# Four convolution layers in one kernel: layer 2's edge columns and masks from GpSimd to ScalarE, and its difference one quarter earlier

## The chip, the cores and the metric

The kernel runs on one core of a Trainium2 chip. The metric is the device time of one execution in microseconds (us), the median of several runs. Engines are named as in the profile: PE is TensorE's matrix products and PEld its weight loads, DVE is VectorE, ACT is ScalarE, POOL is GpSimd, SP is SyncE, which here only issues transfers.

## The reference

The input x has 16 images of 64 channels of 128 x 128 points, float32. Four layers follow each other, each of the form x + layer(gn(x)), where gn normalizes groups of two channels to mean 0 and variance 1:

- layer 0: the Gram matrix of the normalized channels, applied to them, then a 64 x 64 matrix
- layer 1: the absolute values of a horizontal and a vertical 3 x 3 Scharr filter of each channel, summed
- layer 2: a 3 x 3 convolution, 64 to 64 channels, with bias, of an input in which the first 16 channels are shifted one column to the left and the next 16 one column to the right (zeros come in at the edge)
- layer 3: a 3 x 3 and then a 1 x 1 convolution, batch normalization over all 16 images, a clip to 0..255

```python
x = x + _L0_conv_ref(_gn(x), L0_conv_conv_w)
x = x + _L1_conv_ref(_gn(x))
x = x + _L2_conv_ref(_gn(x), L2_conv_W, L2_conv_b)
x = x + _L3_conv_ref(_gn(x), L3_conv_w_bin, ...)
```

## The kernel before

The images go through the layers as a pipeline. One image is cut into eight chunks (NS = 8); a chunk is eight rows of each half of the image for layer 1, and eight pairs of rows for layers 2 and 3. A **step** handles one chunk of each of three images at once: `Front` is layers 0 and 1 of one image, `Layer2` and `Layer3` are those of images some ten steps further back, and `Gram` gathers the Gram matrix of an image still to come. So eight steps make a **cycle**, in which the whole pipeline advances by one image. `starts` gives the step in which each stage begins (15, 25, 35). `both_layers(step)` is true for the steps in which both layer 2 and layer 3 have work.

Each step has four quarters, q = 0 to 3, and within a quarter the stages are called in the order Layer3, Layer2, Front, then `section()` emits TensorE products that are held back, and then "last of q" parts of Layer2 come. All engines are wrapped in `InOrder`: what the program writes first for an engine is what that engine does first. So a call's place in this loop is its place in its engine's queue. The waits between engines are put in by the tile framework.

Layer 2 treats pairs of rows, so that 3 rows x 2 outputs become fewer products. For chunk i+1, in step i:

- `load` brings the rows by six transfers on SyncE's queue into v (tag v2, three buffers). The shift of 32 channels by a column is done by where the transfer reads.
- In quarter 1 ScalarE normalizes them (`v<-v,co` in the profile, 128 x 1154). The shifted channels have wrong columns at the edges. GpSimd first saves what layer 2 has to add at the first and the last column (`edges`, four instructions of 64 x 8), then multiplies both edge columns of v by masks (`keep0`, `keep1`; `v<-v,kc`, two instructions of 128 x 9 or 8).
- `different(i + 1)` lets VectorE form the difference of even and odd rows, d2 (`d2a<-v` and `d2b<-v`, 128 x 1024; two buffers in turn), and GpSimd then issues two transfers that copy d2 into q2, in the other half of the partitions and moved by one column (`q<-d2a`, `q<-d2b`; one buffer). Before step 34 it also copies into the same half, with four transfers.

In step i+1 TensorE uses them: `shared` (quarter 2) multiplies the odd rows into `one` (`one<-v,wi`, a PSUM tile with a single buffer, which layer 3's `one<-v,w` uses in turn); `own` (quarter 3) multiplies d2 into `two` (`two<-d2a,wi`, two buffers, shared with layer 3). `apart_across`, emitted by `section()` of the step before (quarter 1), multiplies q2 into `two`: the products `two<-q,pk` and `two<-q,cross`. They alternate in pairs with layer 3's `two<-d,w`, on other quarters of the array, and the products `po<-x,abd` of layer 0 follow them.

ScalarE adds the bias in reading `one` out (`c<-one,co` for layer 2, `c<-one,b_sb` for layer 3), which frees `one`. VectorE adds the edge columns (`two<-two,edges`) and reads `two` out (`x<-two,c` for layer 2, `y<-two,c` for layer 3), which frees `two`. Of layer 1, VectorE does ten operations per chunk (names u and e), with two Abs by ScalarE between; the last two are `u<-xh,co,u` in quarter 2 and `u<-e,co,u` in quarter 3.

VectorE's order in a full step, before: `u<-xh`, `e<-xh`, `two<-two,edges`, `x<-two,c`, four operations on u and e, `y<-two,c`, layer 3's difference `d<-v`, `u<-xh,co,u`, `u<-e,co,u`, layer 2's difference `d2<-v`. Small operations that work out coefficients stand between them.

Of the kernel before, what the change touches and what calls it, by code (L numbers as in the profile page):

```python
# [11 lines left out]
AF = mybir.ActivationFunctionType  # L12
# [3 lines left out]
B, C, H, W = 16, 64, 128, 128  # L16
# [4 lines left out]
R = 8  # L21
NS = HH // R
# [87 lines left out]
def tile_kernel(ctx: ExitStack, tc: tile.TileContext, x, cw_h, w2_t, b2, wbin_t, w1_t, b1, gamma, beta, consts, out):  # L110
    nc = tc.nc
    pe, dve, act, sp, pool = (InOrder(tc, e) for e in (nc.tensor, nc.vector, nc.scalar, nc.sync, nc.gpsimd))
# [8 lines left out]
    def k(name):  # L121
        return kc[:, AT[name][0]:AT[name][1]]
# [47 lines left out]
    last = [1]  # L170
# [52 lines left out]
    for name in ("d2a", "d2b", "q2", "d3"):  # L223
        t = wpool.tile([P, 2, CP, W + 2], F32, name=name)
# [42 lines left out]
    now = [0]  # L267
# [29 lines left out]
    def coefficients(st, put, back=None):  # L297

        yield
        yield from when(TENSOR)  # L300
        pm = sm(2 * NS)
        small_product(pm, k("gmean"), st.rearrange("p a n -> p (a n)"))
        yield
        co = sv("co", 2) if back is None else sv("co2", 6)
        me = sv("me", 2)
        r, mean = co[:, 0:1], me[:, 0:1]
        yield from rstd(pm, r, me, GN_EPS, None if back is None else co[:, 2:3])
        pool.tensor_scalar(co[:, 1:2], mean, r, -1.0, op0=ALU.mult, op1=ALU.mult)
        if back is not None:

            pool.tensor_add(co[:, 5:6], mean, back)
            pool.tensor_mul(co[:, 3:4], co[:, 2:3], k("left"))
            pool.tensor_mul(co[:, 4:5], co[:, 2:3], k("right"))
        put(co)
# [135 lines left out]
    rows = []  # L450
# [36 lines left out]
    class Gram:  # L487
        first, last = 2, NS + 2
# [4 lines left out]
        def at(self, i, q):  # L493
            b = self.b
            n = 4 * (i - NS) + q

            self.part({1: 44, 5: 42, 9: 42}.get(n, 0))
            if n == 10:
                chains.append(gram_chain(b, self.pg))

            if i == 2 and q == 0:
                for m in range(3):
                    self.load(m)
            m = {11: 0, 13: 1, 15: 2, 19: 3, 21: 4, 23: 5, 27: 6, 31: 7}.get(4 * i + q)
            if m is not None:
                rows_to_columns(b, m, self.xr.pop(m))
                if m + 3 < NS:
                    self.load(m + 3)
# [45 lines left out]
    class Front:  # L554
        first, last = -3, NS
# [182 lines left out]
    def both_layers(step):  # L738

        return starts[0][1] <= step < starts[1][1] + NS * B  # L740
# [60 lines left out]
    def apart_across(two, table, q, m):  # L801

        for kx in range(3):
            for n in range(2):
                o, i = single(table, n)
                w = W - 1 if kx == 2 else W
                wt = cross[cols(1 - i), kx - 1] if kx else packed["pk2"][cols(1 - i), n]
                across.append((
                    two[cols(o), n, 0:m, 0:w], wt, q[cols(1 - i), n, 0:m, kx + 1:kx + 1 + w], kx == 0, kx == 2,
                ))  # L810
# [3 lines left out]
    class Layer2:  # L814
        first, last = -2, NS
# [68 lines left out]
        def at(self, i, q):  # L884
            b = self.b
            closing = i + 1 == NS
            m = CP - 1 if closing else CP
            if q == 0:
                if i == NS:
                    chains.append(coefficients(self.st, self.done))  # L890
                if 1 <= i:
                    two = self.p.pop(i - 1)[0]

                    e = self.edges.pop(i - 1).rearrange("p t (m n) -> p n m t", n=2)
                    ends = two[:, :, :, 0:W:W - 1]
                    dve.tensor_add(ends, ends, e)
                    x3 = ring.tile([P, 2, CP, W], F32, tag="x3", name=f"x3_{b}_{i - 1}", bufs=NS + 2)
                    tiles3[b].append(x3)
                    dve.scalar_tensor_tensor(
                        x3.rearrange("p s j w -> p s (j w)"), two.rearrange("p s j w -> p s (j w)"), 1.0,  # L900
                        self.c.unsqueeze(1).to_broadcast([P, 2, CP * W]),
                        op0=ALU.mult, op1=ALU.add, accum_out=self.st[:, 0, i - 1:i],
                    )
            if q == 1:
                if i == 0:

                    self.wi = stp.tile([P, 2, 3, P], F32, tag="wi", name=f"wi_{b}", bufs=1)
                    for n, base in ((0, w2[:, 2]), (1, wm)):
                        dve.scalar_tensor_tensor(
                            self.wi[:, n].rearrange("p k o -> p (k o)"), k("I3"), self.co[:, 2:3],  # L910
                            base.rearrange("p k o -> p (k o)"), op0=ALU.mult, op1=ALU.add,
                        )
                if -1 <= i < NS - 1:
                    if i == -1:
                        self.co = coefs2.pop(b)
                    t, f = self.v[i + 1], self.whole.pop(i + 1)
                    act.activation(f, f, AF.Identity, bias=self.co[:, 1:2], scale=self.co[:, 0:1])


                    e = stp.tile([P, 2, R], F32, tag="edges", name=f"edges_{b}_{i + 1}", bufs=3)  # L920
                    for side, at in ((0, 0), (1, W + 1)):
                        for rows, j in ((lo, 1), (hi, 0)):
                            n = at + j * W
                            pool.tensor_scalar_mul(
                                e[rows, side], f[rows, n:n + (R - 1) * W + 1:W], self.co[rows, 3 + side:4 + side]
                            )
                    self.edges[i + 1] = e

                    pool.tensor_scalar_mul(t[:, :, 0], t[:, :, 0], k("keep0"))
                    pool.tensor_scalar_mul(t[:, :, W - 1], t[:, :, W - 1], k("keep1"))  # L930
                if i + 2 < NS:
                    self.load(i + 2)
                if 0 <= i < NS:
                    self.two = ps_two.tile([P, 2, CP, W], F32, tag="two", name=f"two2_{b}_{i}")
                    if both_layers(now[0]):
                        apart_across(self.two, TO_SLOTS, q2, m)
            if q == 2:
                if 0 <= i < NS:
                    t = self.v[i]
                    one = ps_one.tile([P, CP, W], F32, tag="one", name=f"one2_{b}_{i}")  # L940
                    two = self.two
                    self.p[i] = two, one
                    shared(one, self.wi[:, 0], t, m)
                    if closing:
                        small_product(one[:, m, :], w0, t[:, R, :])


                if 1 <= i < NS:
                    self.square(i - 1)
                if 1 <= i:  # L950
                    self.store(i - 1)
            if q == 3:
                if 0 <= i < NS:
                    t = self.v.pop(i)
                    two, one = self.p[i]
                    both = self.wi[:, 1]
                    for n in range(2):
                        own(
                            two[:, n], n, TO_SLOTS, w2, d2[i % 2], packed["pk2"],
                            None if both_layers(now[0]) else q2, m, both,  # L960
                        )
                    if closing:
                        p = two[:, 1, m:CP]
                        issue([taps(0, p, [both], [t[:, R:R + 1, :]]), taps(1, p, [both], [t[:, R - 1:R, :]])])
                        p, srcs = two[:, 0, m:CP], [t[:, R - 2:R - 1, :], t[:, R - 1:R, :]]
                        issue([taps(0, p, [w2[:, 0], both], srcs), taps(1, p, [both, w2[:, 1]], srcs)])
            if q == "last of 2" and 0 <= i < NS:
                self.c = ring.tile([P, CP * W], F32, tag="c2", name=f"c2_{b}_{i}", bufs=1)
                act.activation(self.c, flat(self.p[i][1]), AF.Identity, bias=self.co[:, 5:6])
            if q == "last of 0" and i == NS:  # L970
                self.square(i - 1)
            if q == "last of 3" and -1 <= i < NS - 1:
                self.different(i + 1)


    class Layer3:
        first, last = -1, NS
# [142 lines left out]
    for step in range(starts[2][1] - 2, steps):  # L1120
        now[0] = step
        for q in range(4):
            for b in range(B):

                i = step - starts[2][1] - NS * b
# [11 lines left out]
            for b in range(1, B):  # L1137
                at, n = pace[b]
# [28 lines left out]
            if step >= last_one and q == 2:  # L1167

                n = 3 if step == last_one else 1 if step < last_one + NS - 2 else 0
# [29 lines left out]
    e = cpool.tile([P, 1], F32, name="e_bn")  # L1199
# [56 lines left out]
```

## Time and profile before

| | us |
|---|---|
| median of 3 runs | 2649.29 |
| lowest and highest | 2647.46, 2650.26 |
| the profiled execution | 2646.72 |
| its span in the profile | 2645.0 |
| start, until both layers run | 0 to 350 |
| full pipeline with Gram products | 350 to 1583 |
| full pipeline without them | 1583 to 1968 |
| layers 2 and 3 without Front, then layer 3 alone | 1968 to 2200 |
| end: batch normalization and output | 2200 to 2645 |

All engine instructions stand under one line, L73, the helper that records them, so groups are told apart by what they write and read: `out<-in`. A group's row gives the number of instructions, busy time, the mean of one in ns, and the idle time of the engine just before them. A wait's row gives the total, the number of times and the longest. A timeline row gives the start, the duration, and in brackets the idle time of the engine before it with what ended it.

### The profile page before, as it was taken

The numbers are of one execution on the slowest core, as the hardware profiler recorded it, in microseconds if no ns is written. First come the engines' busy times: TensorE is split into PE (matmuls) and PEld (weight loads), VectorE is DVE, ScalarE is ACT, GpSimd is POOL, SyncE is SP. The second block draws the span as 40 slices with busy tenths as digits, with TensorE's granted clock in tenths as the row PEclk, the third lists the DMA queues.
The fourth block names the chain that finished last, engine by engine and source line by source line (L and its number), as shares of the span: only waits on it lengthen the run. The fifth ranks groups of instructions, "written<-read, shape, count | busy, mean of one in ns | idle before, by whom it ended". The sixth has DMA issues, their size and how long they took to land.

```text
span 2645.0 us, 46238 instructions
## 1 busy us (share of the span) xinstructions
PE 2086.3 (79%) x15748; PEld 832.0 (31%) x15748; DVE 2090.4 (79%) x2759; ACT 1787.3 (68%) x2529; POOL 993.3 (38%) x1391
## 2 busy tenths in 40 slices
PE   6568899999999999999999999999999991000000
PEld 4334333434343434343443433333333330000000
DVE  4998899999999999999999999999993335333332
ACT  4766678787878787877878777777774475333332
POOL 3365545343445454444445355555553100000000
PEclk8689899999999999999999999999999995555555
DMA  8799979898888889888979777787767769999999
GB/s 202 204 240 229 222 196 235 209 231 223 231 224 224 221 222 228 218 230 211 238 206 249 196 202 201 193 206 202 208 172 181 204 202 377 419 419 418 419 418 369
DMA packets 682267, 654.53 MB, mean 247 GB/s; under 512 B 56320, under 2 KB 576672, under 8 KB 682032
## 3 DMA queue, kind: packets, MB, share of 16 engines
q1 hardware_dynamic: 668208, 613.83, 80.3%
q0 software_dynamic: 13824, 37.75, 5.5%
q8 instruction: 126, 2.06, 0.3%
q14 instruction: 109, 0.89, 0.1%
HBM read 346.23 MB, written 268.44 MB: 232 GB/s over the span
## 4 chain that ended last, share of the span: by engine, by line
PE 38%; DMA 19%; DVE 2%; ACT 2%; SPq 2%; issue 1%; POOL 0%; DVEq 0%; ACTq 0%; POOLq 0%
PE two L73 21%; PE one L73 13%; SPq L73 2%; PE po L73 2%; PE bank L73 2%; DMA end_x<-x_d 2%; DMA xw<-x_d 2%; DMA xw<-y_d 2%; DMA end_x<-y_d 2%; DMA out<-end_x 2%; DMA out<-xw 1%; DMA out<-end_v 1%; DMA end_u<-x_d 1%; DMA d2b<-y_d 1%; DMA v<-x_d 1%
## 5 line engine op out<-in xcount | busy, mean ns | idle before, releaser
L73 PE MATMUL two<-d,w 64*64 64x512 f32 (+2 forms) x2992 | 697.5, 594 | 0.0
L73 POOL TENSOR_SCALAR edges<-v,co 64x8 f32<-64x8 f32 x512 | 364.2, 711 | 499.6 <-ACT v L73 314.0
L73 PE MATMUL one<-v,w 128*64 128x508 f32 (+2 forms) x1600 | 358.0, 579 | 0.3
L73 PE MATMUL one<-v,wi 128*64 128x508 f32 (+3 forms) x1536 | 353.6, 595 | 0.1
L73 PEld LDWEIGHTS two<-d,w 64*64 64x64 f32 (+1 forms) x2992 | 204.6, 134 | 391.5 <-issue 379.1
L73 DVE SCALAR_TENSOR_TENSOR e<-e 128x1032 f32<-128x1032 f32 (+1 forms) x256 | 313.1, 1223 | 0.0
L73 ACT ACTIVATE xh<-po,co 128x128 f32<-128x128 f32 (+1 forms) x480 | 274.6, 621 | 28.8 <-PE po L73 24.3
L73 PE MATMUL two<-q,cross 64*64 64x508 f32 (+3 forms) x944 | 244.8, 574 | 0.0
L73 PE MATMUL po<-x,abd 64*64 64x512 f32 (+1 forms) x1024 | 205.6, 623 | 48.7 <-ACT xh L73 43.4
L73 DVE SCALAR_TENSOR_TENSOR y<-two,c 128x1024 f32<-128x1024 f32 x128 | 156.0, 1219 | 97.9 <-ACT junk L73 44.7
L73 POOL TENSOR_SCALAR v<-v,kc 128x9 f32<-128x9 f32 x256 | 218.0, 866 | 12.0
L73 ACT ACTIVATE u<-u 128x1024 f32<-128x1024 f32 x128 | 135.3, 1057 | 127.9 <-DVE u L73 127.8
L73 ACT ACTIVATE v<-x,co 128x1024 f32<-128x1024 f32 (+3 forms) x256 | 203.1, 842 | 0.0
L73 ACT ACTIVATE v<-v,co 128x1154 f32<-128x1154 f32 x128 | 171.8, 1342 | 34.4 <-DMA v<-x_d 30.5
L73 DVE TENSOR_TENSOR d<-v 128x1024 f32<-128x1024 f32 x128 | 157.5, 1230 | 47.0 <-ACT v L73 29.2
L73 ACT ACTIVATE c<-one,co 128x512 f32<-128x512 f32 x128 | 87.6, 685 | 157.4 <-PE one L73 156.9
L73 PE MATMUL two<-q,pk 64*64 64x512 f32 (+2 forms) x512 | 175.9, 600 | 14.4 <-DMA q<-d2b 7.9
L73 DVE SCALAR_TENSOR_TENSOR u<-xh 128x1170 f32<-128x1170 f32 x128 | 175.4, 1371 | 10.6 <-DMA x_d<-u 5.4
L73 PE MATMUL two<-d2a,wi 128*64 128x508 f32 (+1 forms) x768 | 183.2, 589 | 0.0
L73 PE MATMUL two<-d2b,wi 128*64 128x508 f32 (+3 forms) x768 | 174.9, 566 | 0.0
L73 PEld LDWEIGHTS one<-v,w 128*64 128x64 f32 x1600 | 111.5, 136 | 190.2 <-issue 172.0
L73 DVE SCALAR_TENSOR_TENSOR u<-xh,co,u 128x1024 f32<-128x1024 f32 x128 | 164.1, 1282 | 8.5 <-ACT u L73 8.5
(174 smaller groups left out, 3744.7 us busy)
## 6 DMA issues: line engine op xcount, KB each, us to landing
x<-in_x SPq DMA_DIRECT2D x256, 256.0 KB, 4.1
x_d<-u SPq DMA_DIRECT2D x512, 128.0 KB, 3.8
y_d<-y SPq DMA_DIRECT2D x512, 128.0 KB, 3.4
x_d<-x SPq DMA_DIRECT2D x496, 128.0 KB, 3.2
xr<-in_x SPq DMA_DIRECT2D x120, 512.0 KB, 5.7
v<-x_d SPq DMA_DIRECT2D x448, 72.1 KB, 2.8
v<-x_d SPq DMA_DIRECT2D x224, 144.2 KB, 2.8
end_x<-x_d SPq DMA_DIRECT2D x39, 512.0 KB, 10.0
```

Source lines behind the costliest of these rows:

```text
L73: return self.tc.keep_in_program_order(call(*args, **kwargs))
```

## The change

Three things are changed in `Layer2.at`. The four edge columns and the two masks of a chunk are done by ScalarE as Copy with a per-partition scale, directly behind its normalization, in place of GpSimd's multiplications. `different(i + 1)` is called in quarter 2, behind `store` and ahead of Front's part of that quarter, for steps in which both layers have work; in other steps it stays at the end of quarter 3. With it go VectorE's difference and GpSimd's transfers into q2. In VectorE's order the difference then stands between `d<-v` and `u<-xh,co,u`.

```diff
                             n = at + j * W
-                            pool.tensor_scalar_mul(
-                                e[rows, side], f[rows, n:n + (R - 1) * W + 1:W], self.co[rows, 3 + side:4 + side]
+                            act.activation(
+                                e[rows, side], f[rows, n:n + (R - 1) * W + 1:W], AF.Copy,
+                                scale=self.co[rows, 3 + side:4 + side],
                             )
                     self.edges[i + 1] = e
 
-                    pool.tensor_scalar_mul(t[:, :, 0], t[:, :, 0], k("keep0"))
-                    pool.tensor_scalar_mul(t[:, :, W - 1], t[:, :, W - 1], k("keep1"))
+                    act.activation(t[:, :, 0], t[:, :, 0], AF.Copy, scale=k("keep0"))
+                    act.activation(t[:, :, W - 1], t[:, :, W - 1], AF.Copy, scale=k("keep1"))
...
                 if 1 <= i:
                     self.store(i - 1)
+                if -1 <= i < NS - 1 and both_layers(now[0]):
+                    self.different(i + 1)
...
-            if q == "last of 3" and -1 <= i < NS - 1:
+            if q == "last of 3" and -1 <= i < NS - 1 and not both_layers(now[0]):
                 self.different(i + 1)
```

## The prediction

> **What bounds the kernel now.** I read the page first (busy shares, the 40 slices), then busy time by window, the waits, and last the timeline of one step. From the page:
>
> ```profile
> PE 2086.3 (79%) x15748; PEld 832.0 (31%) x15748; DVE 2090.4 (79%) x2759; ACT 1787.3 (68%) x2529; POOL 993.3 (38%) x1391
> ...
> PE   6568899999999999999999999999999991000000
> ...
> DVE  4998899999999999999999999999993335333332
> ```
>
> TensorE and VectorE are both nearly full from about 350 to 1960 us; the last fifth, with TensorE idle, is transfers that the change doesn't touch. The windows split the full part in two:
>
> ```profile
> core 0: us, PE busy (x) PEld busy (x) DVE busy (x) ACT busy (x) POOL busy (x), PEclk, DMA share, GB/s
> 350.00:1583.00 1233.00, 1225.51 (x9480) 483.23 (x9478) 1181.17 (x1588) 983.23 (x1447) 572.58 (x817) 1.00 0.86 222
> 1583.00:1968.00 385.00, 383.25 (x2268) 135.30 (x2266) 378.77 (x463) 295.43 (x450) 211.41 (x255) 1.00 0.77 199
> ```
>
> VectorE is busy 95.8% of the first (1181.17 of 1233) and 98.4% of the second. ScalarE is at 80% and 77%. TensorE's 99% is modelled and hides waits, so I asked the waits. Over the whole span, and then VectorE alone from 1583 to 1968:
>
> ```profile
> ACT c L73 <- PE one L73: 245.7, 153, 4.7
> ...
> ACT u L73 <- DVE u L73: 127.8, 82, 4.3
> ...
> PEld two L73 <- DMA q<-d2a: 17.8, 19, 2.7
> PEld two L73 <- DMA q<-d2b: 16.8, 18, 5.4
> ```
>
> ```profile
> DVE x L73 <- DVE two L73: 0.5, 1, 0.5
> DVE y L73 <- ACT u L73: 0.2, 1, 0.2
> ```
>
> The only waits of TensorE that this change can remove are those for q, the copy of layer 2's difference. And in the second window VectorE waits for nothing: 0.7 us in 385. There it alone sets the step, and a TensorE wait for q is only the form that VectorE's lateness takes. A step of the second window takes VectorE 14.49 us from one `u<-xh` to the next, TensorE needs 14.01.
>
> One step, with the wait. It starts at 1186.81 (first weight load of `one<-v,wi`):
>
> ```profile
> 1189.59 1.27 DVE L73 SCALAR_TENSOR_TENSOR u<-xh,co,u 128x1024 f32<-128x1024 f32 x1
> 1190.97 1.28 DVE L73 SCALAR_TENSOR_TENSOR u<-e,co,u 128x1024 f32<-128x1024 f32 x1
> ...
> 1192.18 1.22 DVE L73 TENSOR_TENSOR d2a<-v 128x1024 f32<-128x1024 f32 x1
> ...
> 1196.40 1.23 DVE L73 SCALAR_TENSOR_TENSOR x<-two,c 128x1024 f32<-128x1024 f32 x1 [0.46 <-DVE two L73]
> 1193.96 1.09 POOL L73 DMA_DIRECT2D q<-d2a  x2 [2.89 <-issue]
> 1200.44 0.13 PEld L73 LDWEIGHTS two<-q,pk 64*64 64x64 f32 x1 [2.55 <-DMA q<-d2a]
> ```
>
> The difference follows two operations of layer 1 on VectorE, GpSimd issues two copies behind it, and TensorE waits 2.55 us for the second. This step lasts 17.2 us; the same step of other images takes 14.01.
>
> **What the Trainium skill says.** "ScalarE: Activation LUTs", section "What ACT_TABLE_LOAD costs": an ACTIVATE with immediates takes 186 ns plus 0.833 ns per element, each per-partition pointer adds about 93 ns, and neighbours overlap by about 93 ns. The trace agrees: the 64x128 copy `xh<-pel` takes 285 ns (186 + 107 = 293), the 128x1024 normalization with two pointers 1229 (186 + 186 + 853 = 1225). Section "Table sets: the hidden batching unit": copy, identity and abs are in every set, so the new Copy should load no table; the trace has one table load, 1.28 us, in the whole kernel. "SBUF — State Buffer", section "Who interferes with whom": a VectorE instruction with two SBUF inputs contends with a GpSimd instruction that reads SBUF. In this trace GpSimd is the one that pays: its 64x8 edge columns take 302 ns at best, 711 in the mean and 2470 at worst, while `d<-v` on VectorE takes about 1.22 to 1.23 us with GpSimd busy or not. So VectorE gains next to nothing when GpSimd is emptied.
>
> **Part by part.** The work that moves engines, as it stands on GpSimd and with the nearest ScalarE row:
>
> ```profile
> L73 POOL TENSOR_SCALAR edges<-v,co 64x8 f32<-64x8 f32 x512 | 364.2, 711 | 499.6 <-ACT v L73 314.0 <-DMA x_d<-u 50.6 <-DMA x_d<-x 42.3
> ...
> L73 POOL TENSOR_SCALAR v<-v,kc 128x9 f32<-128x9 f32 x256 | 218.0, 866 | 12.0
> ...
> L73 ACT COPY xh<-pel 64x128 f32<-64x128 f32 x16 | 4.6, 285 | 0.0
> ```
>
> (1) GpSimd loses 582 us of work (364.2 + 218.0) in 128 chunks. It is no bound, so that alone is worth 0. Its queue is then free when the copies are to be issued; only a few issues were late through it (10.1 instead of 7.3 us into the step that starts at 1816).
>
> (2) ScalarE gains six instructions per chunk. One is 186 + 93 + 7 = 286 ns, 193 from start to start. Behind the normalization and behind the edges it waits for its own results and loses the overlap. Sum: 0.02 + (3 x 0.193 + 0.286) + 0.02 + (0.193 + 0.286) = 1.39 us, and I take 1.4 per chunk, 180 in all; 1.2 to 1.75 are the ends (page price without the waits; 0.29 each without overlap). Queued behind them are Abs of u and e, two normalizations `xh<-po`, and `c<-one,co`, which frees the only buffer of `one`; TensorE's next product into it is due 4.77 us into the step. I walked every step from 360 to 2000, taking ScalarE's idle time between the normalization and c off the 1.4. Mostly ScalarE was waiting for VectorE's u or for `one` anyway. What is left pushes c past 4.72 us in about nine steps by 0.2 to 0.9, together 6 us (3.6 at 1.2; 12 at 1.75). VectorE's own use of Abs has 2.3 us of slack and gains 1.15 more from the difference that now stands ahead of it: 0.
>
> (3) The difference moves ahead of `u<-xh,co,u` and `u<-e,co,u`: 1192.18 - 1189.59 = 2.59 us earlier in VectorE's order, same work in sum. It needs the masks: they end 1.4 us after the normalization, in the latest case 1.9 us into the step, where the difference would now start at 3.3. No wait. Layer 1's two operations come 1.15 us later; their results go to SyncE's queue, which in the middle of the kernel stores them some 6 to 9 us after they are ready.
>
> (4) Both copies of q go with it on GpSimd's queue, 2.59 us earlier; they land 3.5 to 7.4 us (median 4.8) after the difference, in the trace of before. TensorE needs the second at 10.49 us into a step. Its landings against each step's first weight load: in 48 of 105 steps from 360 to 1970 it lands later, 51 us in sum, 31 before 1583 and 20 after. Less 2.59 us each, 2 us remain.
>
> (5) What is late next: `x<-two,c`, which frees the buffer that those products write. It stands in VectorE's order where it stood. In the shown step it ends at 1197.63, 10.82 us in, and the products could have started from 10.43. So of the 2.55 us about 0.4 stays as a wait for VectorE.
>
> The sum for 350 to 1583. It runs in cycles of eight steps (one image). Mean of nine cycles from 422.0 to 1548.6: 125.2 us. The shortest step of each kind gives TensorE 122.5; VectorE without its waits needs 122.1. Both are near 122.5, and what costs is the coupling: in the five short steps VectorE falls behind by about 4.1 us (0.5 to 1.8 per step), in the three with Gram products (17 us) it catches up. x allows a lag about 1.24 us short of that, so 1.24 per cycle stays. Excess now: 9 x 2.7 = 24, and 5 more from 360 to 420: 29. Left after: 9.5 x 1.24 = 12 by VectorE, 6 by ScalarE. **Gain 11.** From 1583 to 1968: 0, VectorE paces. From 1968 on TensorE runs without waits for q: 0. Before 350, with edges and masks alone changed, VectorE no longer waits 0.2 to 1.3 us for masks (5.5 in all), but ScalarE is back to back there in half the steps, with TensorE and VectorE waiting for it; I take **1 us lost**, from 4 gained to 5 lost. Sum: -10. The profiled execution took 2646.72 us (span 2645.0), so 2636.7; the median of the runs is 2.6 higher, so **2639**.
>
> **Rivals.** *A, the forecast*: q's wait goes, VectorE and ScalarE take back over half. 2639, between 2624 and 2644. Chance 0.52.
> *B, same*: VectorE paces the first window too, x ends every wait that q ended, or the copies don't land earlier. For it: 95.8% busy, x ends within 0.8 us of the first q in most late steps. Against: VectorE does wait some 30 us for y in that window, and y is free to start when TensorE's last product into `two` ends. 2647. Chance 0.27.
> *C, slower*: ScalarE becomes the bound. Place: c of layer 2 in the short steps, and the steps before 350. Without ScalarE's part the sum is 29 - 12 - 1 = 16 us gained. My walk gives 12 us of waits for c at 1.75 us a chunk, 26 at 2.2, 46 at 2.7: it decides from about 1.9 (0.32 an instruction, no overlap at all and more). At 2.2 the result is 10 us slower, 2659. For it: ScalarE has no idle time from the normalization to c in one step of eight. Against: it has 20% in the window. Chance 0.17.
> *D*: all 29 come, with no new wait: 2620. Chance 0.04.
> That the change doesn't do what it says I count in B; the built order shows the difference moved in 110 of 128 chunks, with TensorE's and SyncE's orders unchanged.
>
> **The numbers.** 0.2% is 5.3 us, about what a measurement of this kernel can tell from no change. Faster: A and D, 0.56; same 0.27; slower 0.17. The range takes A and B whole with the lightest part of C: 2622 to 2656.
>
> **What would show it.** Right: edges at 0.28 to 0.30 us on ScalarE; waits of PEld for q under 5 us in sum; q issued about 4 us into the step instead of 7; step cycles near 124 before 1583; steps of 14.5 after it as before. Wrong: PEld waiting for `ACT c` by more than 15 us, ScalarE's small instructions at 0.4 or more, VectorE waiting for `ACT u` or `ACT v`, or cycles still at 125.

## The result and the profile after

The changed kernel takes 2629.55 us in the median of six runs (2625.40 to 2637.24), beside 2647.25 us for the kernel before in the same comparison: a ratio of 0.9938, 95% interval 0.9925 to 0.9951. That is 17.7 us less, 0.62%. The profiled execution took 2633.98 us, 12.7 less than the profiled one of before and one of the longer of its six.

The page of the changed kernel, the rows shown of before and ScalarE's slices:

```profile
PE 2068.1 (79%) x15748; PEld 822.4 (31%) x15748; DVE 2085.6 (79%) x2759; ACT 1988.8 (76%) x3297; POOL 410.9 (16%) x623
...
PE   6578899999999999999999999999999990000000
...
DVE  4998989999999999999999999999994335333332
ACT  4778889898989898989989888888986575333332
```

GpSimd lost 582 us, as stated. ScalarE gained 201 us and now stands at eight or nine tenths in every slice of the full part. The same two windows:

```profile
core 0: us, PE busy (x) PEld busy (x) DVE busy (x) ACT busy (x) POOL busy (x), PEclk, DMA share, GB/s
350.00:1583.00 1233.00, 1218.88 (x9514) 472.88 (x9512) 1182.76 (x1589) 1108.41 (x1931) 230.97 (x345) 1.00 0.86 222
...
1583.00:1968.00 385.00, 379.52 (x2266) 136.99 (x2267) 379.25 (x464) 338.76 (x605) 60.09 (x98) 1.00 0.78 199
```

ScalarE has 90% in the first, up from 80%. The waits over the span (who waits, for whom: us, times, longest), and VectorE's only wait of the second window:

```profile
ACT c L73 <- PE one L73: 134.4, 84, 4.3
...
PEld one L73 <- ACT c L73: 37.7, 48, 2.1
ACT u L73 <- DVE u L73: 33.0, 28, 3.5
```

```profile
DVE y L73 <- ACT v L73: 0.2, 1, 0.2
```

Of the rows `PEld two <- DMA q` (35 us before) 0.3 us are left. Instead TensorE waits for c, which it hardly did (0.6 us in PEld's row before). Where ScalarE had waited for `one` (246 us) and u (128 us), it now waits 134 and 33: its slack is spent. The step shown of before, in the timeline of the changed kernel; it starts at 1182.02, again the first weight load of `one<-v,wi`:

```profile
1185.07 1.22 DVE L73 TENSOR_TENSOR d2a<-v 128x1024 f32<-128x1024 f32 x1
...
1186.21 1.28 DVE L73 SCALAR_TENSOR_TENSOR u<-xh,co,u 128x1024 f32<-128x1024 f32 x1
...
1186.85 1.11 POOL L73 DMA_DIRECT2D q<-d2a  x2 [9.19 <-issue]
1187.30 0.68 ACT L73 ACTIVATE c<-one,co 128x512 f32<-128x512 f32 x1
...
1188.03 2.78 PE L73 MATMUL one<-v,w 128*64 128x512 f32 x12 [0.66 <-ACT c L73]
...
1193.33 0.14 PEld L73 LDWEIGHTS two<-q,pk 64*64 64x64 f32 x2
```

The difference starts 3.05 us into the step (5.37 before), the copies of q are issued at 4.8 us (7.15 before), the products on q start with no wait, and the new wait, for c, stands earlier. The step takes 14.88 us instead of 17.2.

To place the gain I took from each trace the first weight load of `one<-v,wi` of chunk n, counted over all images. n = 12 lies at about 360 us, 16 to 88 are nine cycles of the first window, 88 to 118 take in the whole second (in the trace of before they run from 1549 to 1991). Each row is one profiled execution; those of e4, e5, e8 and e10 are the longest of their runs, e3's is the shortest, e6 has no other. The experiments are described below.

| kernel | to n = 12 | 12 to 16 | a cycle, 16 to 88 | 88 to 118 | span |
|---|---|---|---|---|---|
| before | 359.5 | 62.5 | 125.18 | 442.0 | 2645.0 |
| changed, first profile | 355.7 | 62.1 | 124.72 | 438.9 | 2632.2 |
| changed, second (e11) | 356.1 | 60.4 | 123.92 | 438.5 | 2623.4 |
| e1 ScalarE's part alone | 359.0 | 61.5 | 125.38 | 444.6 | 2646.6 |
| e2 the move alone | 359.8 | 62.1 | 126.34 | 454.1 | 2666.7 |
| e3 no edges, no masks | 350.9 | 60.4 | 123.89 | 438.4 | 2618.2 |
| e4 masks on GpSimd | 357.1 | 60.4 | 125.97 | 440.5 | 2645.5 |
| e5 ScalarE's part twice | 367.9 | 61.3 | 131.13 | 445.8 | 2708.4 |
| e6 edges by half | 355.7 | 60.4 | 126.11 | 438.5 | 2642.5 |
| e7 half the move | 360.7 | 61.6 | 124.41 | 442.7 | 2638.5 |
| e8 one copy | 355.4 | 62.2 | 123.82 | 439.3 | 2624.8 |
| e9 behind Gram | 353.9 | 60.5 | 123.94 | 439.1 | 2622.8 |
| e10 no addition | 356.8 | 59.9 | 126.03 | 429.6 | 2633.8 |

### The profile page after: what moved, and what is told of

Read it like the earlier page. It is cut to its first block, busy times and chain, and to the rows that moved or that the text cites. A ratio compares the mean times of both kernels' runs of the same rounds, so it can differ in the third digit from the quotient of the medians.

```text
span 2632.2 us, 45566 instructions
## 1 busy us (share of the span) xinstructions
PE 2068.1 (79%) x15748; PEld 822.4 (31%) x15748; DVE 2085.6 (79%) x2759; ACT 1988.8 (76%) x3297; POOL 410.9 (16%) x623
## 4 chain that ended last, share of the span: by engine, by line
PE 45%; DMA 23%; DVE 11%; ACT 9%; SPq 7%; issue 3%; POOL 0%; DVEq 0%; ACTq 0%; POOLq 0%
PE two L73 23%; PE one L73 15%; SPq L73 7%; DVE u L73 4%; PE bank L73 3%; PE po L73 3%; ACT v L73 2%; DVE e L73 2%; DMA v<-x_d 2%; DMA end_x<-x_d 2%; DMA out<-end_x 2%; DMA x_d<-u 2%; DMA x<-in_x 2%; DMA out<-xw 2%; DMA end_x<-y_d 2%
## 5 line engine op out<-in xcount | busy, mean ns | idle before, releaser
L73 PE MATMUL one<-v,wi 128*64 128x508 f32 (+3 forms) x1536 | 350.9, 591 | 0.0
L73 PE MATMUL po<-x,abd 64*64 64x512 f32 (+1 forms) x1024 | 189.5, 623 | 49.8 <-ACT xh L73 46.5
L73 PE MATMUL two<-q,cross 64*64 64x508 f32 (+3 forms) x944 | 216.1, 573 | 0.0
L73 POOL DMA_DIRECT2D q<-d2b x138 | 72.1, 526 | 721.5 <-DVE d2b L73 412.9
L73 POOL DMA_DIRECT2D q<-d2a x138 | 73.8, 537 | 642.1 <-issue 276.1
L73 DVE SCALAR_TENSOR_TENSOR u<-e,co,u 128x1024 f32<-128x1024 f32 x128 | 164.2, 1283 | 8.2 <-DVE u L73 0.5
L73 DVE SCALAR_TENSOR_TENSOR x<-two,c 128x1024 f32<-128x1024 f32 x128 | 156.7, 1225 | 14.5 <-ACT junk L73 0.5
L73 ACT ACTIVATE edges<-v,co 64x8 f32<-64x8 f32 x512 | 156.3, 305 | 11.0 <-POOL co L73 0.9
```

Of the source, the lines that this page charges most:

```text
L73: return self.tc.keep_in_program_order(call(*args, **kwargs))
```

## The experiments

**e1 and e2: each half alone.**

Against the changed kernel, e1 first:

```diff
-                if -1 <= i < NS - 1 and both_layers(now[0]):
-                    self.different(i + 1)
...
-            if q == "last of 3" and -1 <= i < NS - 1 and not both_layers(now[0]):
+            if q == "last of 3" and -1 <= i < NS - 1:
```

```diff
-                            act.activation(e[rows, side], ..., AF.Copy, ...)
+                            pool.tensor_scalar_mul(e[rows, side], ...)
...
-                    act.activation(t[:, :, 0], ...)
-                    act.activation(t[:, :, W - 1], ...)
+                    pool.tensor_scalar_mul(t[:, :, 0], ...)
+                    pool.tensor_scalar_mul(t[:, :, W - 1], ...)
```

> The edge columns and masks on ScalarE as in the changed kernel, the difference left at the end of the step. Theory (both halves of the change act in different stages): before 350 us and from 1583 to 1968, where the difference's place does not matter or VectorE paces, this kernel should keep the changed kernel's 3 to 4 us each, and from 350 to 1583 it should lose about 6 us to ScalarE, with TensorE's waits for q still 30 to 50 us in sum: 2640 to 2648 us in all. Rival (it was the emptied GpSimd queue that got the copies of q out sooner): the waits for q fall below 15 us without the move, and the time is that of the changed kernel, about 2630. Rival (ScalarE's load is a cost everywhere): slower than before, 2653 or more.

> The difference moved to the third quarter, the edge columns and masks left on GpSimd. In the kernel before the masks end 3.3 to 4.6 us into a step in most steps, and the moved difference starts at about 3.3. Theory (the two halves need each other): VectorE now waits for GpSimd's masks, 0 to 1.3 us in a step, about 0.5 in the mean; where VectorE paces (1583 to 1968, 27 steps) that costs some 13 us, before it most of what the earlier q brings: 2640 to 2660 us. Rival (the move alone makes the gain and ScalarE's part only costs): no waits of VectorE for GpSimd above 5 us in sum, and with ScalarE 1.4 us a chunk lighter the time is below the changed kernel's, 2618 to 2625.

e1: 2643.02 us beside 2645.92, ratio 0.9995 (0.9982 to 1.0008): no difference. The waits of TensorE's weight loads for q from 350 to 1583 are those of before, shown first, then e1's:

```profile
PEld two L73 <- DMA q<-d2a: 15.8, 15, 2.7
...
PEld two L73 <- DMA q<-d2b: 2.7, 4, 0.9
```

```profile
PEld two L73 <- DMA q<-d2a: 16.4, 18, 2.3
...
PEld two L73 <- DMA q<-d2b: 2.2, 4, 0.9
```

So an empty GpSimd queue does not bring q sooner in this window; the rival falls. The gain that I gave this half before 350 and after 1583 was not in its profile (2648.38 us, above its median) as a whole: 0.5 us to n = 12, and a loss after 88, where one cycle took 121.2 us (117.5 before; 4.4 us of waits for `q<-d2b`).

e2: 2668.64 us, ratio 1.0086 (1.0073 to 1.0099): 22.7 us slower, beyond my 2660. VectorE's waits over the span, among them:

```profile
DVE d2b L73 <- POOL v L73: 26.1, 52, 1.2
...
DVE d2a L73 <- POOL v L73: 22.7, 52, 1.3
```

That is 49 us in 104 steps, 0.47 in the mean: the mechanism expected, with more of it lost. TensorE's weight loads hardly wait for q in its first window (0.5 us for `q<-d2a`, nothing for `q<-d2b`), and all the same it loses in both windows: 1.2 us in a cycle and 12 us from n = 88 to 118. **One half alone brings nothing, the other loses 22.7, both together gain 17.7.** The move needs masks that are done where the difference now stands, about 3 us into the step; e7 tests that.

**e3: the six instructions left out.**

```diff
+    noedge = stp.tile([P, 2, R], F32, tag="noedge", name="noedge", bufs=1)
+    pool.memset(noedge, 0.0)
...
-                            act.activation(e[rows, side], ...)
-                    self.edges[i + 1] = e
+                    self.edges[i + 1] = noedge
...
-                    act.activation(t[:, :, 0], ...)
-                    act.activation(t[:, :, W - 1], ...)
```

> The changed kernel without the six small instructions on any engine: the edge columns are a constant zero tile and nothing is masked, so this part of the computation is left out. The difference stands in the third quarter. It prices the six instructions on ScalarE. Theory (the prediction's size): they cost 6 us from 350 to 1583 and 0 to 5 elsewhere, so 2620 to 2625 us. Rival (ScalarE has become the next bound): the changed kernel's trace has 48 us of TensorE's waits for c; if these are lost time and not slack taken elsewhere, 2585 to 2600. Rival (VectorE paces all of it now): no difference to the changed kernel, 2627 to 2632.

2623.68 us, ratio 0.9928 (0.9911 to 0.9945): 5.9 us below the changed kernel's median in its own comparison and 4.6 below that of e11, with intervals of the ratios that overlap. So not 30 or 40 us: of the 37.7 us of PEld waits for c most cost nothing.

**e4: the masks back on GpSimd, edges on ScalarE.**

```diff
-                    act.activation(t[:, :, 0], t[:, :, 0], AF.Copy, scale=k("keep0"))
-                    act.activation(t[:, :, W - 1], t[:, :, W - 1], AF.Copy, scale=k("keep1"))
+                    pool.tensor_scalar_mul(t[:, :, 0], t[:, :, 0], k("keep0"))
+                    pool.tensor_scalar_mul(t[:, :, W - 1], t[:, :, W - 1], k("keep1"))
```

> The changed kernel with the two masks back on GpSimd, behind ScalarE's edge columns: ScalarE's addition falls from 1.4 to about 0.95 us a chunk. Theory (TensorE's waits for c are ScalarE's price): these fall from 48 to about 30 us in sum; the masks end about 1.5 us later than in the changed kernel and still ahead of the difference in nearly every step, so the time is 2 to 5 us below the changed kernel's, about 2626. Rival (the masks' lateness is what counts): VectorE waits for GpSimd's v before the difference, more than 10 us in sum, and the time is 2635 to 2645.

2633.44 us, ratio 0.9952 (0.9939 to 0.9965): no better than the changed kernel. TensorE's waits for c, PEld's and PE's together, stayed at 46.9 us (48.5 in the changed kernel) where 30 were expected, and VectorE waited about 6 us for GpSimd's masks. Neither expectation holds. Its profiled execution (2647.57) was its longest, so I read no more from it.

**e5: every small instruction twice.**

```diff
                             act.activation(e[rows, side], ...)
+                            act.activation(e[rows, side], ...)
...
                     act.activation(t[:, :, 0], ...)
                     act.activation(t[:, :, W - 1], ...)
+                    act.activation(t[:, :, 0], ...)
+                    act.activation(t[:, :, W - 1], ...)
```

> The changed kernel with each of the six small instructions issued twice in a row (the second time they write the same values). The block between the end of layer 2's normalization and the end of the masks, 1.83 us a chunk in the changed kernel's trace, grows to about 3.6. It prices more ScalarE time at this place. Theory (a wait for c is taken back for about two thirds by slack elsewhere: the kernel without the six instructions was 5.9 us faster in the medians, against waits for c of 38 us): another 1.75 us a chunk is past all slack in the short steps and costs 15 to 30 us, so 2645 to 2660. Rival (linear: as much again as the first six cost): about 2636. Rival (no slack takes it back, every us of lateness in the five short steps is lost): 105 steps, some 60 of them short, 1.75 us each, 2700 or more.

2708.29 us, ratio 1.0226 (1.0212 to 1.0241). The number of the third expectation came (2700 or more), and my theory missed by some 50. Not quite every us counts: a cycle is 7.2 us longer than in e11, where 1.75 us in each of five short steps would be 8.75. Window and waits from 350 to 1583:

```profile
350.00:1583.00 1233.00, 1169.86 (x9214) 449.90 (x9212) 1135.17 (x1527) 1171.00 (x2280) 212.94 (x325) 0.99 0.82 213
```

```profile
PEld one L73 <- ACT c L73: 90.0, 46, 3.3
...
DVE y L73 <- ACT edges L73: 43.3, 34, 2.0
...
DVE d2b L73 <- ACT v L73: 16.2, 16, 1.6
```

ScalarE is 95% busy, TensorE waits for c, and VectorE's differences wait for the masks (`d2b` 16.2 us, `d2a` 4.6). The row `DVE y <- ACT edges` has to be read with care: y reads neither edges nor masks, and in 32 of these 34 waits the (modelled) end of TensorE's last product into `two` lies 0.10 us ahead of y. So y waits for TensorE, and the name in the row is only what else ended shortly before. **The price of ScalarE time is not linear**: the first 1.84 us per chunk cost about 5 us in all (e3), the next 1.75 cost 79. The bend lies between a block of 1.84 and one of 3.59 us; no run places it closer.

**e6: the four edge instructions in another order.**

```diff
-                    for side, at in ((0, 0), (1, W + 1)):
-                        for rows, j in ((lo, 1), (hi, 0)):
+                    for rows, j in ((lo, 1), (hi, 0)):
+                        for side, at in ((0, 0), (1, W + 1)):
```

> The changed kernel with the four edge instructions in another order: both sides of the lower 64 partitions, then both of the upper 64, where the changed kernel alternates. In its trace they start 0.32 us apart and do not overlap, while the two masks on 128 partitions start 0.20 to 0.22 apart. Theory (an instruction on other partitions than the one before does not overlap with it): two of the three distances fall to about 0.20 us, and the block from the normalization's end to the masks' end from 1.83 to 1.6 us. Rival (instructions on 64 partitions never overlap here): all stay at 0.32. The time is within 5 us of the changed kernel's either way.

ScalarE's timeline around one normalization, the changed kernel first, then e6 (start, duration, a merged row for instructions of one group):

```profile
1082.26 1.35 ACT L73 ACTIVATE v<-v,co 128x1154 f32<-128x1154 f32 x1 [0.68 <-DMA v<-x_d]
1083.65 1.26 ACT L73 ACTIVATE edges<-v,co 64x8 f32<-64x8 f32 x4
1084.94 0.51 ACT L73 ACTIVATE v<-v,kc 128x9 f32<-128x9 f32 x2
```

```profile
1085.19 1.35 ACT L73 ACTIVATE v<-v,co 128x1154 f32<-128x1154 f32 x1 [0.79 <-DMA v<-x_d]
1086.57 1.01 ACT L73 ACTIVATE edges<-v,co 64x8 f32<-64x8 f32 x4
1087.62 0.51 ACT L73 ACTIVATE v<-v,kc 128x9 f32<-128x9 f32 x2
```

From the end of the normalization to the end of the masks it is 1.84 us and 1.59. Start to start, the edges stand 0.32, 0.315, 0.32 us apart in the changed kernel and 0.214, 0.304, 0.210 here: two neighbours on the same 64 partitions overlap by some 0.09 us, two on different halves do not. The Trainium skill, "ScalarE: Activation LUTs", section "What ACT_TABLE_LOAD costs", gives the overlap of 93 ns for neighbours and names no such condition; here it holds only within the same partitions. An instruction that writes again what its neighbour just wrote does not overlap either: in e5 the repeated edges start 0.34 us after the first. The one run of e6 took 2644.33 us and is not compared: its first window has 39.4 us of ScalarE's waits for layer 2's input (`ACT v <- DMA v<-x_d`), beside 14.7 in the first profile of the changed kernel and none in its second (e11).

**e7: half the move, edges and masks on GpSimd.**

The edges and masks as in e2; the call moved from quarter 2 to the head of Layer 2's quarter 3:

```diff
-                if -1 <= i < NS - 1 and both_layers(now[0]):
-                    self.different(i + 1)
...
             if q == 3:
+                if -1 <= i < NS - 1 and both_layers(now[0]):
+                    self.different(i + 1)
```

> Edge columns and masks on GpSimd as in the kernel before, the difference moved by half the way: between layer 1's operations u<-xh,co,u and u<-e,co,u, so 1.28 us earlier than before and 1.3 later than in the changed kernel. Theory (the move alone loses only because the difference there comes before GpSimd's masks are done, 49 us of VectorE's waits in the run with the move alone): here the masks are done when it starts in nearly all steps, VectorE's waits for GpSimd's v fall below 10 us, the waits for q fall from 27 to 5 to 12 us, and the time is 2637 to 2643 us, between before and the changed kernel. Rival (with GpSimd full, the copies of q go out late wherever the difference stands): waits for q stay above 20 us and the time is before's, 2646. Rival (any move with masks on GpSimd loses): 2655 or more.

2640.51 us, ratio 0.9974 (0.9960 to 0.9989): the theory's 2637 to 2643. VectorE's waits for the masks and PEld's for q, from 350 to 1583:

```profile
DVE d2a L73 <- POOL v L73: 2.9, 11, 0.5
DVE d2b L73 <- POOL v L73: 2.2, 10, 0.2
```

```profile
PEld two L73 <- DMA q<-d2b: 1.9, 3, 1.1
PEld two L73 <- DMA q<-d2a: 0.7, 3, 0.3
```

So it is the place of the difference in VectorE's order that brings q in time, also with GpSimd as full as before, if the masks are done by then. Half the distance already takes PEld's waits for q in this window from 18.5 to 2.6 us. From n = 88 to 118 it gains nothing (442.7).

**e8: one copy instead of four scaled edges on ScalarE.**

```diff
-                    for side, at in ((0, 0), (1, W + 1)):
-                        for rows, j in ((lo, 1), (hi, 0)):
-                            n = at + j * W
-                            act.activation(e[rows, side], ...)
+                    sides = stp.tile([P, 2, R + 1], F32, tag="sides", name=f"sides_{b}_{i + 1}", bufs=2)
+                    act.copy(sides, bass.AP(tensor=f.tensor, offset=f.offset, ap=[list(f.ap)[0], [W + 1, 2], [W, R + 1]]))
+                    for rows, j in ((lo, 1), (hi, 0)):
+                        pool.tensor_mul(
+                            e[rows], sides[rows, :, j:j + R], self.co[rows, 3:5].unsqueeze(2).to_broadcast([C, 2, R])
+                        )
```

> The changed kernel with ScalarE's part cut to three instructions a chunk: one copy of both edge columns of all partitions (128x18) in place of the four scaled ones, and the two masks; GpSimd, off the path, scales the copied columns in two instructions. The output is the same. The block from the normalization's end to the masks' end falls from 1.83 to about 0.8 us. Theory (what ScalarE's six instructions cost is their time ahead of c): TensorE's waits for c fall from 38 to about 15 us, and the time comes to 2624 to 2627, between the changed kernel and the one without edges and masks (2623.7). Rival (a quarter less on ScalarE made no difference with the masks on GpSimd, so its length is not what counts but DMA landings are): as the changed kernel, 2629 to 2632. Rival (GpSimd's instructions now delay the copies of q): waits for q come back above 10 us, 2635 or more.

2625.02 us (2622.73 to 2626.60), ratio 0.9911 (0.9897 to 0.9925), as expected. ScalarE's timeline:

```profile
951.13 1.35 ACT L73 ACTIVATE v<-v,co 128x1154 f32<-128x1154 f32 x1
952.57 0.22 ACT L73 COPY sides<-v 128x18 f32<-128x18 f32 x1
952.82 0.52 ACT L73 ACTIVATE v<-v,kc 128x9 f32<-128x9 f32 x2
```

0.86 us instead of 1.84. PEld's waits for c from 350 to 1583 fall from 27.2 to 3.5 us, and eight of the nine cycles take 123.88 to 123.95 us. It beats before clearly; beside the changed kernel it is 3 to 5 us lower in the medians, with ratio intervals that meet or overlap.

**e9: the difference behind the Gram statistics.** On e8:

```diff
-                if -1 <= i < NS - 1 and both_layers(now[0]):
+                if -1 <= i < NS - 1 and both_layers(now[0]) and i != 3:
                     self.different(i + 1)
...
             if q == 3:
+                if i == 3 and both_layers(now[0]):
+                    self.different(i + 1)
```

> The kernel with one copy of the edge columns, and the difference of every chunk's step with i = 3 moved half the way only, so that it stands behind VectorE's small operations on the Gram product (g, st, junk) there. In the run with one copy TensorE waits 1.46 us for junk in each cycle at this point (11 us in eight cycles), since the moved difference, 1.14 us, stands ahead of them; the cycles take 123.9 us, the shortest steps of each kind sum to 122.5. Theory A (the moved difference delays the Gram statistics, and that is the rest): the wait goes, cycles of about 123.0, and 6 to 9 us less in all, 2617 to 2619. Theory B (VectorE is behind by that much after its five short steps whatever stands first, the prediction's 1.24 us per cycle; the wait only moves to x or q): cycles stay at 123.7 to 124.2 and the time at 2624 to 2627.

2623.43 us, ratio 0.9908 (0.9892 to 0.9925), cycles of 123.79 to 124.31: theory B, since the wait moved and the cycles stayed. In e8 TensorE's weight load waits for junk:

```profile
960.92 0.20 PEld L73 LDWEIGHTS bank<-st,kc 128*64 128x64 f32 x4 [1.46 <-DVE junk L73]
```

In the same step of e9 it waits 0.32 there, and 0.48 later, until x ends:

```profile
963.08 1.23 DVE L73 SCALAR_TENSOR_TENSOR x<-two,c 128x1024 f32<-128x1024 f32 x1
...
964.38 0.17 PEld L73 LDWEIGHTS two<-q,pk 64*64 64x64 f32 x2 [0.48 <-issue]
```

The bracket says "issue"; x, which frees the buffer, ends at 964.31, 0.07 us ahead.

**e10: VectorE lighter by one operation.** On e3:

```diff
-                    dve.tensor_add(ends, ends, e)
```

> As the run without edges and masks, and without VectorE's addition of the edge columns (two<-two,edges, 0.17 us a step), so this part is left out too. It makes VectorE 0.17 us a step faster and nothing else. Theory (VectorE paces from 1583 to 1968, and its lag over five short steps is the rest before that): 0.17 x 27 = 4.6 us less after 1583, and 0.17 x 5 = 0.85 us less in each of nine and a half cycles, 8 us: 2611 instead of 2623.7. Rival (TensorE's own order sets the cycles before 1583): only the 4.6 us, 2619. Rival (TensorE paces everywhere): 2622 to 2625.

2628.70 us (2619.45 to 2635.58), ratio 0.9924 (0.9905 to 0.9944): not faster than e3, which no theory expected. The sum hides two opposite parts. From n = 88 to 118 it gains 8.8 us on e3: there VectorE paces, as forecast. I had put 4.6, because I priced the addition by its 0.17 us of busy time; x waits for it, and in e3's steps from 1713 to 1743 x starts 1.44 us after `e<-xh`, in e10's 1.15. That is 0.29 us a step, and 30 steps make 8.7. Before n = 88 its profile loses: one cycle of 122.53 us, then cycles of 124.9 to 128.8. Waits from 350 to 1583:

```profile
ACT v L73 <- DMA v<-x_d: 67.2, 39, 4.1
```

```profile
DVE u L73 <- DMA x_d<-u: 23.7, 12, 4.8
```

In e3 the first is 0.7 us and the second absent. Layer 2's input, and the stores that free layer 1's buffer u, arrive late in those cycles. This is not shown to come of a lighter VectorE: the profile is the longest of e10's six runs beside the shortest of e3's, and e6 has 39.4 us of the first wait with VectorE 95% busy. No run took the transfers away.

**e11: the changed kernel once more.**

> The changed kernel once more, for a second profiled execution beside the first (2634 us, where the median was 2629.6) and a comparison on the chip of this call. Theory (single executions differ by how often layer 2's input and layer 1's stores land late, with ScalarE too full to absorb it): the median is again 2628 to 2632 while cycles of eight steps from 420 to 1550 us differ among themselves by 1 to 3 us, where they stay within 0.1 us with one copy. Rival (the excess sits in fixed steps): the same cycles are long by the same amounts as in the first profile.

2628.26 us (2624.83 to 2640.78), ratio 0.9932 (0.9911 to 0.9953). Its second profiled execution is 8.8 us shorter than the first, and from n = 24 on its cycles are even, 123.83 to 123.90. TensorE's waits for c are all there:

```profile
PEld one L73 <- ACT c L73: 20.9, 30, 1.8
```

The difference goes with the transfers: from 350 to 1583 the first profile has 14.7 us of `ACT v <- DMA v<-x_d` and 5.1 of `DVE u <- DMA x_d<-u`, the second has neither. So the excess does not sit in fixed steps, and the rival falls; the uneven cycles that the theory expected stand in the first profile alone. What makes the transfers late in one execution and not in another stays open.

## Why the prediction was right, and where not

The sign was right, and in the first window the mechanism too; the gain was 17.7 us instead of 10. With the two profiles of the changed kernel averaged, the table divides 17.2 us of it: 9.0 from n = 12 to 88, where the forecast had 11; 3.6 before, where it had 1 lost; 3.4 from n = 88 to 118 and 1.2 after, where it had nothing. So nearly half of the gain came from stages in which the prediction saw none. These parts rest on one profile of before and are sure to some us only.

Of the signs named beforehand, q's waits under 5 us (0.3 in PEld's rows) the cycles near 124 and the steps of 14.5 in the second window (14.47 in the median) came. The edges took 305 ns, not 280 to 300, and q was issued 4.8 us into the step shown, not about 4. One sign of being wrong came as well: PEld waited 37.7 us for c, where more than 15 was to mean a loss. Point 2 says why it was a poor sign.

1. **GpSimd emptied, worth 0.** Alone, yes (e1 with ScalarE's part: 0.9995). But it was wrong to cost the two halves one by one: without fast masks the move loses 22.7 us (e2).
2. **ScalarE, 1.4 us per chunk and 6 us of waits for c.** Both mis-sized. The block is 1.84 us, above my upper end of 1.75: a 64 x 8 edge with a pointer takes 305 ns where I had 286, and the four stand 0.32 apart where I had 0.193, since they alternate between halves (e6). The waits for c in the first window are 27.2 us by PEld's row and 8.2 by PE's, not the 6 of my walk nor its 12 at 1.75. Yet the six instructions cost about what I had given, 5 us in the medians (e3; the intervals overlap). That the numbers meet is luck, since they do not cost it at those waits: e11's cycles with them equal e3's without them (123.92 and 123.89). In e11 the step with index 1 of each cycle is 0.32 us longer than in e3 and the next 0.40 shorter. So what a wait for c costs in one step is given back in the next; I take it that it stands in for a wait that VectorE would have imposed there. My walk counted every such wait as lost. Between the profiles of e3 and e11 the whole difference, 5.2 us, lies before n = 12 (350.9 and 356.1). That does not size the six instructions there either: e10, without them too, stands at 356.8.
3. **Difference and q, 51 us of lateness down to 2.** Right: no q wait is left in the first window of the changed kernel, and e7 shows that the place in VectorE's order does it.
4. **x next, 1.24 us per cycle stays.** Right, the best term of the forecast: 122.5 + 1.24 = 123.74, and e3, e8, e9 and e11 stand at 123.8 to 123.9. That it agrees to 0.2 us is partly luck: the very shortest step of each kind in these nine cycles of before adds up to 121.9, the 14.01 that the prediction names for the step shown stands only after 1549 us (the shortest of its kind before that is 14.56), and the working does not show how 1.24 came about. In e9 the wait moves and the cycle stays, which speaks for VectorE's lag and against any particular instruction. The form differs: in the changed kernel it mostly shows as `PEld bank <- DVE junk` (11.0 us, 8 times), since the moved difference stands ahead of the Gram statistics, which I did not list among what is queued behind it.
5. **First window, gain 11.** In e11's execution the nine cycles take 11.4 us less than before, in the first profile 4.2; the rest of that profile went with late transfers. But the profile of before has such waits too (16.7 us of `ACT v <- DMA v<-x_d` in this window), so 11.4 compares an execution with late transfers and one without. I had costed layer 1's later results at nothing, behind stores that follow 6 to 9 us after; the first profile has 5.1 us of waits for those stores, so that cover is thin.
6. **Before 350, 1 lost.** Wrong sign in the profiles: 3.8 and 3.5 us earlier at n = 12. VectorE's waits for the masks went as stated, but ScalarE's cost there seems smaller than the 6.5 I had set against them. Up to n = 10 (321 us in before) the difference is not moved, so e1 has the same order there, and it came only 0.5 us earlier. One wait for q at about 300 us alone varies, 5.4 us in before, 3.9 and 0.8 in the two profiles, 1.6 in e1. So a single execution does not size this stage.
7. **1583 to 1968, 0.** 3.2 and 3.5 us were gained from n = 88 to 118. In the first 26 of these 30 steps VectorE's time without idle is 0.9 and 1.1 us less, its idle time 0.5 and 0.7 less. The other 1.8 us lie in the last four. The last of them, in which VectorE no longer paces (5.1 us idle in before), takes 14.28 us before, with 0.7 us of waiting for q, and 13.25 in the changed kernel. Why VectorE's own time fell is not settled. That VectorE paces in this window is shown by e10.

Of the rivals, C (ScalarE as the bound) did not come, but its price is real: 1.75 us more per chunk made the kernel 79 us slower (e5). Its threshold of 1.9 us was set by the walk, and the block lies at 1.84, so by the prediction's own reckoning little of the gain would have been left; that it still gains is due to point 2, which the prediction did not know. B fell with the q waits. D's 2620 is below even the changed kernel's shortest run.

## What to carry to other kernels

Cost the parts of a change together where one is what another waits for: here each alone was worth nothing or less. A new wait in the profile is a price only if the time behind it is not taken by a slower engine anyway; compare the sum over a cycle, not the wait. And when an engine has to take over small work on a tight path, give it the smallest form (one plain copy of 0.22 us instead of four scaled ones over 1.26) and leave the rest to the engine that was emptied. In e8 that took nearly all of TensorE's waits for c away; that it is faster than the changed kernel is likely (3 to 5 us) but not clear of noise.

## What was not expected of the hardware

- Neighbouring ScalarE instructions on the same 64 partitions start 0.21 us apart (e6) unless the second writes again what the first wrote (0.34, e5), on alternating halves 0.32; on all 128 the two masks start 0.215 apart.
- A 128 x 18 copy on ScalarE takes 223 ns, less than a scaled 64 x 8 one at 305.
- Executions of one kernel differ by up to 16 us (2624.83 to 2640.78) with the same program, and the two traces of it differ in when transfers of layer 2's input and layer 1's stores land. Less work on ScalarE does not settle it: e8's four runs lie within 4 us, but those of e3, with less still, within 15 (2620.00 to 2635.38).
